# Where a step's four gathers stand among its TensorE tasks: all at once, or one by one behind a product

## The chip, the cores and the metric

The kernel runs on one NeuronCore of a Trainium2 chip. A core has five engines, each with a queue of its own that is worked off in order: TensorE (PE in the profile, its weight loads PEld), VectorE (DVE), ScalarE (ACT), GpSimd (POOL) and SyncE (SP). They share an on-chip memory (SBUF), the accumulators of the matmuls (PSUM) and 16 DMA engines, and wait for each other by semaphores. What counts is the device time of one execution in microseconds; the median of several runs is compared.

## The reference

Everything is float32. A layer of a graph network over 6250 nodes of 256 features and 100000 edges (to which every node's edge to itself is added) is followed by a mixture of experts:

```python
# graph layer, added to x
xn = layer_norm(layer_norm(x))
h = (xn @ W).reshape(N, 8, 32)
e = leaky_relu(a_src[src] + a_dst[dst], 0.2)          # one score per edge and head
alpha = exp(e - max over the edges of dst) / (sum over the edges of dst)
agg = segment_sum(h[src] * alpha[:, :, None], dst)
out = layer_norm(agg + xn @ W_res + bias)
x = x + out + gelu_tanh(out @ ffn_w1 + ffn_b1) @ ffn_w2 + ffn_b2      # 256 -> 1024 -> 256
# mixture of experts, added to x
t = layer_norm(x)
top_p, top_idx = top_k(softmax(t @ Wr + br), 2)       # two of eight experts
y[e] = gelu(ln_e(t) @ W1[e] + b1[e]) @ W2[e] + b2[e]  # 256 -> 1024 -> 256
x = x + sum over the two of (top_p / sum(top_p)) * y[top_idx]
```

The edges come sorted by their target `dst`; the sources `src` are random. So every edge needs the row of its source node, wherever that lies.

## The kernel before

**Edge steps.** A first part of the program writes a table `tab_s` to DRAM, one row per node: 256 features and 16 numbers from which the edge's weight comes (1088 bytes). Then the edges are worked off in 196 steps. A step has four tiles (`G = 4`) of 128 edges, one edge per partition. For each tile, `fetch` (L838 to L848) issues one gather on POOL: an indirect DMA that brings the 128 rows named by a column of `srce` into a quarter of the buffer `gs`. The pool of `gs` has four buffers, so the gathers of a step can start when `weigh`, four steps earlier, has read its buffer.

The rest of a step's work is spread over the steps behind it, so that every engine has something of another step to do. This is the list, worked from left to right once per step; the number says how many steps behind `fetch` a stage runs:

```python
    STAGES = ((sum_up, 6), (weigh, 3), (add_tiles, 4), (place, 4), (turn_spread, 1), (give, 2),
              (spread, 0), (add_nodes, 5), (fetch, 0))
```

- `spread` (DVE) makes a 0/1 matrix `oh` from each edge's place among 32 target nodes; `turn_spread` transposes it on PE (`pt`, L867); `give` (PE, `pz`, L875) multiplies it with the targets' numbers `qd`, so each edge gets its target's.
- `weigh` (DVE) reads the gathered rows: `ww` (L883), the maximum of two halves (L886) and `msg` (L887), the rows times the weights. It is the last that reads `gs`.
- `add_tiles` (PE, `pl`, L902) sums the messages of four tiles by target; behind the last step of a group of nodes, `add_nodes` (PE) and `sum_up` (DVE, `acc_lo`, `acc_hi`) add the group to the nodes' sums.

**Tasks.** Beside the edge steps runs everything that comes behind them: for nodes whose edges are all done, the residual, LayerNorm and the feed-forward network (node units); the routing and the scatter of the tokens' rows to the experts' lists in DRAM (`scatter`, L1437, two indirect DMAs per tile on POOL, each followed by a memset, L1448); and, as soon as an expert's list holds a block of 256 rows, that block's network. Each piece is a `Task` with an engine, a cost and the tasks that it depends on. `block_unit` makes an experts' block: `note` (DVE), `turn` (PE, transposes to `turned_in`), eight `up` (PE, `ph`, L1018, followed by the activation `ht` on ACT, L1021), eight `down` (PE, `py`, L1028), `finish` (DVE, `yb`, L1540), `weigh_block` (ACT) and two `give_back` (POOL, L1550), indirect DMAs that add the 128 rows of a tile to the output. `py` has one PSUM buffer, held from the first `down` to `finish`. Its weights (`w1b`, `w2b`, 1 MB each) and its rows `xb` are loaded by SP. The list `blocks` gets an entry for each experts' block when its tasks are made.

**What sets the order.** The whole loop is traced under `tc.manual_schedule()`: an engine's queue has its instructions in the order in which the Python code emits them. Once per step the stages are emitted, and then `run_tasks` (L974 to L991) hands out tasks in the order of `pending` until the budgets are used up, `ROOM = {"PE": 7.5, "DVE": 7.6, "ACT": 5.0, "POOL": 2.6, ...}` in microseconds, less what the stages take (`EDGES`, `BEHIND`). A POOL task costs 2.6, so that there is at most one in a step. As `fetch` is the last stage, POOL's queue has, for each step, the four gathers and then the step's POOL task, if there is one. Between the engines only data and free buffers set the order: a gather waits for nothing of its own step.

Of the kernel before, what the change touches and what calls it, by code (L numbers as in the profile page):

```python
# [45 lines left out]
F32 = mybir.dt.float32  # L46
# [8 lines left out]
P = 128  # L55
# [6 lines left out]
G = 4  # L62
# [160 lines left out]
def gnn_moe_kernel(  # L223
# [28 lines left out]
    nc = tc.nc  # L252
# [5 lines left out]
    KD = D // P  # L258
    KF = F // P
# [4 lines left out]
    DT = D + 2 * H  # L264
# [6 lines left out]
    while EP < ET:  # L271
        m = 8
# [16 lines left out]
    order = [(q, i) for q in range(NQ - 1, -1, -1) for i in range(groups[q][1])]  # L289
# [47 lines left out]
    tab_s = dp.tile([NP + P, DT], F32, name="tab_s")  # L337
# [20 lines left out]
    srce = gp.tile([P, EP], I32, name="srce")  # L358
# [126 lines left out]
    with ExitStack() as actx:  # L485
# [42 lines left out]
        for i in range(2):  # L528
# [3 lines left out]
                                    axis=AX.X, op=ALU.add)  # L532
# [26 lines left out]
        for k in range(KD):  # L559
            nc.tensor.matmul(pb.rearrange("p a h -> p (a h)"), ones,  # L560
                             gb[:, k].rearrange("p a h -> p (a h)"), start=k == 0,
                             stop=k == KD - 1)
# [24 lines left out]
        for i0, t0 in enumerate(starts):  # L587
# [16 lines left out]
            for j in range(n):  # L604
                t = t0 + j
# [14 lines left out]
                ph = aps.tile([P, WC], F32, name="ph")  # L620
                for k in range(KD):
                    nc.tensor.matmul(ph, xt[:, j, k, :], wc[:, k, :], start=k == 0,
                                     stop=k == KD - 1)
# [16 lines left out]
            for tab, r0, r1 in ((tab_q, 0, LOWR), (tab_h, HB, NP // 4)):  # L640
                a0, a1 = max(m0, r0), min(m1, r1)
                if a0 < a1:
                    nc.gpsimd.dma_start(tab[a0 - r0:a1 - r0], bass.AP(
                        tensor=tab_d.tensor, offset=tab_d.offset + a0 * 4 * 2 * H,
                        ap=[[4 * 2 * H, a1 - a0], [1, W32 * 2 * H]]))
# [3 lines left out]
            for a, k0, b0, b1 in ((acc_lo, 0, t0, min(t1, KHI + 2)),  # L649
                                  (acc_hi, KHI, max(t0, KHI + 2), t1)):  # L650
                if b0 < b1:
                    m, i = b1 - b0, slice(b0 - t0, b1 - t0)
# [172 lines left out]
    bg = edges.enter_context(tc.tile_pool(name="bg", bufs=4))  # L825
# [5 lines left out]
    live = {}  # L831

    def step_tiles(s, a):
# [2 lines left out]
        t0, m = groups[q]  # L836
        return a[:, t0:t0 + G * m].rearrange("p (j m) -> p j m", m=m)[:, :, i]

    def fetch(s):
        gs = bg.tile([P, G, DT], F32, name="gs")  # L840
        q, i = order[s]
        t0, m = groups[q]
        for j in range(G):
            t = t0 + j * m + i
            nc.gpsimd.indirect_dma_start(  # L845
                out=gs[:, j, :], out_offset=None, in_=tab_s,
                in_offset=bass.IndirectOffsetOnAxis(ap=srce[:, t:t + 1], axis=0))
        live[s, "gs"] = gs  # L848

    def spread(s):  # L850

# [20 lines left out]
    def give(s):  # L872

        pz = bps.tile([P, G * 2 * H], F32, name="pz", bufs=2)
        nc.tensor.matmul(pz, live.pop((s, "oht")), live[order[s][0], "qd"].rearrange(  # L875
            "p j c -> p (j c)"), start=True, stop=True)
        live[s, "pz"] = pz

    def weigh(s):
# [51 lines left out]
    def sum_up(q):  # L931
# [4 lines left out]
        for b in range(2):  # L936
# [4 lines left out]


    STAGES = ((sum_up, 6), (weigh, 3), (add_tiles, 4), (place, 4), (turn_spread, 1), (give, 2),
              (spread, 0), (add_nodes, 5), (fetch, 0))
    LASTST = 6

# [26 lines left out]

    def run_tasks(s, room):  # L974

        more = True
        while more:
            more = False
            for t in list(pending):
                if (t.take in held or room[t.eng] <= 0.0  # L980
                        or any(d.step is None or d.step + gap > s for d, gap in t.deps)):
                    continue
                pending.remove(t)
                t.step = s
                room[t.eng] -= t.cost
                if t.take:
                    held.add(t.take)
                if t.free:
                    held.remove(t.free)
                t.fn()  # L990
                more = True  # L991

    def back(tasks, n):

        return tasks[-n:][:1] if len(tasks) >= n else []
# [18 lines left out]
    def up(c, env, w1, func, b):  # L1014
        W = env["n"] * P
        ph = cps.tile([P, 2 * P], F32, name="ph", bufs=2)
        for k in range(KD):
            nc.tensor.matmul(ph[:, :W], w1[:, k, c * P:(c + 1) * P], env["in"][:, k, :W],  # L1018
                             start=k == 0, stop=k == KD - 1)
        ht = cw.tile([P, 2 * P], F32, name="ht", bufs=2 * KF)  # L1020
        nc.scalar.activation(ht[:, :W], ph[:, :W], func, bias=b[:, c:c + 1], scale=1.0)  # L1021
        env["ht", c] = ht

    def down(j, c0, c1, env, w2):
        if j == 0 and c0 == 0:
            env["py"] = cps.tile([P, 2, D], F32, name="py")
        for c in range(c0, c1):
            nc.tensor.matmul(env["py"][:, j, :], env["ht", c][:, j * P:(j + 1) * P], w2[:, c, :],  # L1028
                             start=c == 0, stop=c == KF - 1)

    turns, downs_, ups_ = [], [], []

# [2 lines left out]
    def net(env, src, deps, w1, w2, func, b, more=(), scale=None, more2=()):  # L1035

        n = env["n"]
        tn = task(lambda: turn(src(), "in", env, scale and scale()), "PE", 0.3 * n,
                  [*deps, *[(d, 0) for d in back(ups_, 2)]])
        free = [(d, 0) for d in back(downs_, 2)]  # L1040
        ups = [task(lambda c=c: up(c, env, w1(), func, b()), "PE", 0.46 * n, [tn, *more, *free])
               for c in range(KF)]
        dn = []
        for j in range(n):
            for c in range(0, KF, 2):
                dn.append(task(lambda j=j, c=c: down(j, c, c + 2, env, w2()), "PE", 0.92,
                               [(dn[-1], 0)] if dn else [ups[-1], *more2],
                               take=None if dn else "py"))
        if not urgent:
            before = [t for t in waiting if t.step is None]  # L1050
            for t in before:
                pending.remove(t)
            every = KF // len(before) if before else 1
            for i, t in enumerate(before):
                pending.insert(pending.index(ups[min((i + 1) * every, KF) - 1]) + 1, t)
            waiting[:] = dn
        turns.append(tn)
        ups_.append(ups[-1])
        downs_.append(dn[-1])
        return dn[-1]  # L1060
# [544 lines left out]
    blocks, stored, cleared, sure, chunked, moew, last_hi, ahead = [], [], [], [], [0], [], [], []  # L1605
# [6 lines left out]
    s, u, since, was_nodes, loaded = 0, 0, [], False, {}  # L1612

    with tc.manual_schedule():
        nc.sync.dma_start(xs[E * CAP:, :].rearrange("(p r) d -> p r d", r=2),
                          blank[:, None, :].to_broadcast([P, 2, DX]))
        while s < NG + LASTST or pending or u < len(units) or len(blocks) < NS:
# [47 lines left out]
            room = dict(ROOM if s < NG + LASTST else ROOM_AFTER)  # L1665
            if s < NG + LASTST:
                g = s - 5
                ends = 0 <= g < NG and order[g][1] == groups[order[g][0]][1] - 1
                for e in EDGES:
                    room[e] -= EDGES[e] + ends * BEHIND[e]  # L1670
            run_tasks(s, room)
            s += 1
            if there is None and final_list and final_list[0].step is not None and len(blocks) > NS - 2:
                there = nc.values_load(total[0:1, 0:1], min_val=0, max_val=NX)
        if NS < NX:
            with tc.If(there > NS):
                while pending or len(blocks) < NX:
                    nb = len(blocks) + len(ahead)
                    if len(ahead) < 2 and nb < NX:
                        block_loads(nb)  # L1680
                    if ahead:
                        block_unit(*ahead.pop(0))
                    run_tasks(s, dict(ROOM_AFTER))
                    s += 1
# [31 lines left out]
```

## Time and profile before

| | |
|---|---|
| median of 6 runs | 1831.66 us (1828.84 to 1833.26) |
| the profiled execution | 1829.86 us, span from its first to its last instruction 1828.1 us |
| PE, PEld busy | 1595.8 us (87%), 1239.2 us (68%) |
| DVE, ACT, POOL busy | 1064.8 us (58%), 707.6 us (39%), 1140.3 us (62%) |
| mean granted TensorE clock | 0.945 of full speed |
| gathers (L845) | 784, 817.3 us on POOL, 1043 ns each |
| DMA | 348.12 MB, 190 GB/s on average |

The profile is one execution on the chip. The edge steps end at about 1520 us of the span; in the steps from about the 75th on, with experts' blocks among the tasks, a step takes some 7.1 us. A line of the groups names the line of code, the engine, the operation, the program's names of the output and the inputs, how many there are, the busy time, the mean of one in ns, and the idle time of the engine just ahead of them with what ended most of it (`<-issue`: nothing that the profile shows). A line of the timeline gives the start and the duration in us; the idle time ahead stands in brackets. "DVE ww L883 <- DMA gs" in the waits reads: DVE's instruction of line 883 waited for the DMA that fills `gs`. The time that an indirect DMA takes on POOL is the time in which POOL makes its descriptors; the data land later.

### The profile page before, as it was taken

The numbers are of one execution on the slowest core, as the hardware profiler recorded it, in microseconds if no ns is written. First come the engines' busy times: TensorE is split into PE (matmuls) and PEld (weight loads), VectorE is DVE, ScalarE is ACT, GpSimd is POOL, SyncE is SP. The second block draws the span as 40 slices with busy tenths as digits, with TensorE's granted clock in tenths as the row PEclk, the third lists the DMA queues.
The fourth block names the chain that finished last, engine by engine and source line by source line (L and its number), as shares of the span: only waits on it lengthen the run. The fifth ranks groups of instructions, "written<-read, shape, count | busy, mean of one in ns | idle before, by whom it ended". The sixth has DMA issues, their size and how long they took to land. (4 is left out here: it accounts for less than half of the span.)

```text
span 1828.1 us, 28283 instructions
## 1 busy us (share of the span) xinstructions
PE 1595.8 (87%) x8479; PEld 1239.2 (68%) x8479; DVE 1064.8 (58%) x3809; ACT 707.6 (39%) x1623; POOL 1140.3 (62%) x1190
## 2 busy tenths in 40 slices
PE   5756986878787799999999999999998999999996
PEld 4533664656555577777777777777776777788885
DVE  6757878888888866675766575546344445030000
ACT  4731323233232344444444444444432343443332
POOL 4347754757666667767787777777777774222222
PEclk9977887989888899999999999999999999999998
DMA  6897644546554746667657666777676768847661
GB/s 187 263 264 246 199 142 136 152 138 173 159 155 132 234 154 199 188 183 195 202 163 222 189 191 208 212 211 222 198 223 198 228 178 252 256 110 211 186 220 40
DMA packets 246639, 348.12 MB, mean 190 GB/s; under 512 B 45992, under 2 KB 202824, under 8 KB 246476
## 3 DMA queue, kind: packets, MB, share of 16 engines
q1 hardware_dynamic: 184220, 203.16, 34.4%
q0 software_dynamic: 58944, 139.58, 28.9%
q10 hardware_dynamic: 3312, 3.48, 0.6%
q8 instruction: 70, 1.15, 0.3%
q14 instruction: 93, 0.76, 0.1%
HBM read 282.76 MB, written 67.52 MB: 192 GB/s over the span
## 5 line engine op out<-in xcount | busy, mean ns | idle before, releaser
L845 POOL DMA_INDIRECT gs<-tab_s,srce x784 | 817.3, 1043 | 331.2 <-issue 196.8
L1018 PE MATMUL ph<-turned_in,w1b 128*128 128x256 f32 (+1 forms) x1696 | 419.8, 378 | 16.6 <-ACT turned_in L1010 9.5
L1028 PE MATMUL py<-w2b,ht 128*128 128x256 f32 x1648 | 416.4, 383 | 7.7 <-DVE yb L1540 7.2
L1018 PEld LDWEIGHTS ph<-turned_in,w1b 128*128 128x128 f32 x1696 | 312.8, 191 | 67.6 <-ACT turned_in L1010 15.0
L1021 ACT ACTIVATE ht<-ph,pc 128x256 f32<-128x256 f32 (+1 forms) x424 | 197.6, 467 | 404.8 <-PE ph L1018 404.3
L1028 PEld LDWEIGHTS py<-w2b,ht 128*128 128x128 f32 x1648 | 310.5, 192 | 50.8 <-DVE yb L1540 9.0
L1550 POOL DMA_INDIRECT out_dram<-yb,tos x103 | 166.3, 1615 | 224.8 <-ACT ht L1021 80.3
L887 DVE TENSOR_TENSOR msg<-gs,msg 128x1024 f32<-128x1024 f32 x196 | 240.7, 1228 | 6.7
L1018 PE MATMUL ph<-turned_in,w_sb 128*128 128x256 f32 (+1 forms) x800 | 197.4, 388 | 3.6 <-ACT ht L1021 3.3
L1028 PE MATMUL py<-w_sb,ht 128*128 128x256 f32 x784 | 194.5, 390 | 6.1 <-DVE xin L1119 4.1
L883 DVE TENSOR_TENSOR ww<-gs,pz 128x64 f32<-128x64 f32 x196 | 42.2, 215 | 234.4 <-DMA gs<-tab_s,srce 145.7
L1028 PEld LDWEIGHTS py<-w_sb,ht 128*128 128x128 f32 x784 | 151.3, 196 | 29.1 <-DVE xin L1119 4.9
L1018 PEld LDWEIGHTS ph<-turned_in,w_sb 128*128 128x128 f32 x800 | 150.6, 198 | 28.9 <-ACT ht L1021 5.6
L1021 ACT ACTIVATE ht<-ph,prm 128x256 f32<-128x256 f32 (+1 forms) x200 | 93.2, 469 | 166.0 <-PE ph L1018 165.5
L1540 DVE TENSOR_TENSOR yb<-py,b2b 128x512 f32<-128x512 f32 (+1 forms) x53 | 35.7, 673 | 178.7 <-PE py L1028 172.4
L927 PE MATMUL p<-part,oh 128*128 128x264 f32 x220 | 82.9, 461 | 64.5 <-DVE acc_hi L938 51.8
L902 PE MATMUL pl<-msg,oh 128*32 128x264 f32 x1568 | 132.4, 410 | 6.8 <-DVE msg L887 6.7
L1437 POOL DMA_INDIRECT xs<-xe,slot x98 | 104.7, 1069 | 45.5 <-issue 19.4
L906 ACT ACTIVATE part<-pl 128x264 f32<-128x264 f32 x110 | 42.8, 389 | 195.8 <-PE pl L902 193.5
L938 DVE SCALAR_TENSOR_TENSOR acc_lo<-p,here,acc_lo 128x264 f32 x112 | 55.2, 493 | 97.9 <-PE p L927 80.6
L867 PEld LDWEIGHTS pt<-ident,oh 128*128 128x128 f32 x196 | 27.6, 141 | 115.4 <-issue 62.7
L1199 PE MATMUL py<-wres,xtf 128*128 128x256 f32 x196 | 73.3, 539 | 34.6 <-DVE rg L1205 21.5
(338 smaller groups left out, 1925.5 us busy)
## 6 DMA issues: line engine op xcount, KB each, us to landing
w1b<-in_L_ffn_W_dram SPq DMA_DIRECT2D x53, 1024.0 KB
w2b<-in_L_ffn_W_dram SPq DMA_DIRECT2D x53, 1024.0 KB
xb<-xs SPq DMA_DIRECT2D x50, 260.0 KB
gs<-tab_s,srce POOLq DMA_INDIRECT x784
b2b<-in_L_ffn_b_dram SPq DMA_DIRECT2D x53, 128.0 KB
tab_s<-hg SPq DMA_DIRECT2D x12, 544.0 KB
xg<-in_x_dram SPq DMA_DIRECT2D x12, 512.0 KB
xt_d<-xt SPq DMA_DIRECT2D x12, 512.0 KB
```

What stands on the lines that cost most here:

```text
L845: nc.gpsimd.indirect_dma_start(out=gs[:, j, :], out_offset=None, in_=tab_s, in_offset=bass.IndirectOffsetOnAxis(ap=srce[:, t:t + 1], axis=0))
L887: nc.vector.tensor_tensor(msg[:, :, :D].rearrange("p t (h d) -> p t h d", h=H), gs[:, :, :D].rearrange("p t (h d) -> p t h d", h=H), msg[: ...
L902: nc.tensor.matmul(pl[j * W32:(j + 1) * W32, :], oh[:, j, :], msg[:, j, :], start=i == 0, stop=last)
L906: nc.scalar.activation(part, pl, AF.Copy)
L927: nc.tensor.matmul(p2, oh2, part, start=True, stop=True)
L938: nc.vector.scalar_tensor_tensor(to, p2, here[:, b, q:q + 1], to, op0=ALU.mult, op1=ALU.add)
L1018: nc.tensor.matmul(ph[:, :W], w1[:, k, c * P:(c + 1) * P], env["in"][:, k, :W], start=k == 0, stop=k == KD - 1)
L1021: nc.scalar.activation(ht[:, :W], ph[:, :W], func, bias=b[:, c:c + 1], scale=1.0)
L1028: nc.tensor.matmul(env["py"][:, j, :], env["ht", c][:, j * P:(j + 1) * P], w2[:, c, :], start=c == 0, stop=c == KF - 1)
L1199: nc.tensor.matmul(py[:, j, :], env["xt"][:, j, k, :], wres[:, k, :], start=k == 0, stop=k == KD - 1)
L1437: st = nc.gpsimd.indirect_dma_start(out=xs, out_offset=bass.IndirectOffsetOnAxis(ap=slots[k][:n, t:t + 1], axis=0), in_=xes[u // 2][:n, pl ...
L1550: st = nc.gpsimd.indirect_dma_start(out=out, out_offset=bass.IndirectOffsetOnAxis(ap=tos[:, b, j:j + 1], axis=0), in_=env["yb"][:, j, :], ...
```

## The change

`fetch` emits only the first gather of a step in its place and puts the other three on a list `later`. `run_tasks` emits one of them after a task each time another quarter of the step's PE budget is used up, and what is left behind the last task. Further, each gather gets a dependency on the last product traced ahead of it (`pace[-1]`: `give`'s product, or the last matmul of an `up` or a `down`): POOL may issue it when this product is done. Both hold once `blocks` isn't empty, from step 69 on; ahead of that the four gathers are emitted at once as before, and have no such dependency. The order in which the other engines' instructions are emitted is unchanged; on POOL, a step's `give_back` or `scatter` now comes between the first gather and those behind it, wherever it is handed out ahead of them.

```diff
+    pace, later = [], []
+
     def fetch(s):
-        gs = bg.tile([P, G, DT], F32, name="gs")
+        live[s, "gs"] = bg.tile([P, G, DT], F32, name="gs")
+        gather(s, 0)
+        later.extend(lambda j=j: gather(s, j) for j in range(1, G))
+        if not blocks:
+            while later:
+                later.pop(0)()
+
+    def gather(s, j):
+
         q, i = order[s]
         t0, m = groups[q]
-        for j in range(G):
-            t = t0 + j * m + i
-            nc.gpsimd.indirect_dma_start(
-                out=gs[:, j, :], out_offset=None, in_=tab_s,
-                in_offset=bass.IndirectOffsetOnAxis(ap=srce[:, t:t + 1], axis=0))
-        live[s, "gs"] = gs
+        t = t0 + j * m + i
+        ld = nc.gpsimd.indirect_dma_start(
+            out=live[s, "gs"][:, j, :], out_offset=None, in_=tab_s,
+            in_offset=bass.IndirectOffsetOnAxis(ap=srce[:, t:t + 1], axis=0))
+        if blocks:
+            tc.add_manual_dep(ld.ins, pace[-1].name, mybir.DependencyInfo(
+                mybir.DependencyClass.Sync, mybir.DependencyReason.DATA),
+                reason="the gathers come one by one")
...
     def give(s):
...
-        nc.tensor.matmul(pz, live.pop((s, "oht")), live[order[s][0], "qd"].rearrange(
+        mm = nc.tensor.matmul(pz, live.pop((s, "oht")), live[order[s][0], "qd"].rearrange(
             "p j c -> p (j c)"), start=True, stop=True)
+        pace[:] = [mm.ins]
...
     def run_tasks(s, room):
 
+        whole = room["PE"]
...
                 t.fn()
                 more = True
+                if later and room["PE"] <= whole * len(later) / G:
+                    later.pop(0)()
+        while later:
+            later.pop(0)()
```

In `up` and `down` the last matmul is put into `pace` in the same way.

More of the change, by code (lines that the diff above doesn't have):

```diff
@@ L1017, in up @@
         for k in range(KD):
-            nc.tensor.matmul(ph[:, :W], w1[:, k, c * P:(c + 1) * P], env["in"][:, k, :W],
-                             start=k == 0, stop=k == KD - 1)
+            mm = nc.tensor.matmul(ph[:, :W], w1[:, k, c * P:(c + 1) * P], env["in"][:, k, :W],
+                                  start=k == 0, stop=k == KD - 1)
+        pace[:] = [mm.ins]
         ht = cw.tile([P, 2 * P], F32, name="ht", bufs=2 * KF)
@@ L1027, in down @@
         for c in range(c0, c1):
-            nc.tensor.matmul(env["py"][:, j, :], env["ht", c][:, j * P:(j + 1) * P], w2[:, c, :],
-                             start=c == 0, stop=c == KF - 1)
+            mm = nc.tensor.matmul(env["py"][:, j, :], env["ht", c][:, j * P:(j + 1) * P],
+                                  w2[:, c, :], start=c == 0, stop=c == KF - 1)
+        pace[:] = [mm.ins]
     turns, downs_, ups_ = [], [], []
```

## The prediction

> **What bounds the kernel now.** I read the busy times first, then four stretches of the stage that the change touches, then POOL's groups and its timeline, then the chain of events at the place where PE waits longest.
>
> The page's busy row and its row of the gathers:
>
> ```profile
> PE 1595.8 (87%) x8479; PEld 1239.2 (68%) x8479; DVE 1064.8 (58%) x3809; ACT 707.6 (39%) x1623; POOL 1140.3 (62%) x1190
> ...
> L845 POOL DMA_INDIRECT gs<-tab_s,srce x784 | 817.3, 1043 | 331.2 <-issue 196.8
> ```
>
> The stretches (window, length, then busy us and instructions of PE, PEld, DVE, ACT, POOL; then clock, DMA share, GB/s):
>
> ```profile
> 640.00:806.00 166.00, 157.89 (x892) 123.35 (x891) 113.02 (x415) 76.70 (x163) 116.42 (x117) 0.99 0.59 174
> 806.00:1140.00 334.00, 321.47 (x1811) 253.61 (x1808) 213.51 (x757) 147.98 (x320) 264.38 (x264) 0.99 0.67 200
> 1140.00:1520.00 380.00, 357.27 (x2022) 279.64 (x2021) 177.36 (x555) 145.15 (x325) 298.76 (x273) 0.99 0.71 208
> ```
>
> PE is 94 to 96% busy: it is the bound. But POOL, in the two lower rows, has hardly anything left. Its groups between 806 and 1520 us show why (busy, mean ns, then idle time before and its releasers):
>
> ```profile
> L845 POOL DMA_INDIRECT gs<-tab_s,srce x406 | 430.5, 1060 | 121.7 <-issue 105.3 <-DMA gs<-tab_s,srce 4.0 <-DVE ww L883 2.4
> L1550 POOL DMA_INDIRECT out_dram<-yb,tos x54 | 88.4, 1637 | 19.9 <-issue 10.2 <-ACT ht L1021 3.4 <-DMA out_dram<-yb,tos 2.3
> L1437 POOL DMA_INDIRECT xs<-xe,slot x38 | 40.6, 1069 | 9.4 <-issue 8.4 <-DVE rsh L468 0.3 <-DVE pc L1523 0.3
> ```
>
> Ahead of nearly every one of these 498 instructions lies the same gap, whatever releaser is named: 453 of 0.30 or 0.31 us and 38 of 0.19, behind a memset, are 143.5 of the 149 us idle by the timeline. So POOL is full from 806 to 1520: 3.4 us of real waiting, at 7 instructions, in 714. What it loses there it doesn't win back. Ahead of 806 it is not full: its last real wait is for a free buffer.
>
> ```profile
> 803.10 0.98 POOL L845 DMA_INDIRECT gs<-tab_s,srce  x1 [4.36 <-DVE msg L887]
> 804.38 1.82 POOL L845 DMA_INDIRECT gs<-tab_s,srce  x1 [0.30 <-issue]
> ```
>
> The waits between 1140 and 1520 (us in all, times, longest) show who suffers when POOL is late; from 640 to 900 us DVE has no such wait.
>
> ```profile
> DVE ww L883 <- DMA gs<-tab_s,srce: 133.7, 34, 9.8
> ...
> PE py L1028 <- DVE yb L1540: 5.8, 2, 5.1
> ```
>
> And the place where it reaches PE:
>
> ```profile
> 1381.89 0.95 POOL L845 DMA_INDIRECT gs<-tab_s,srce  x1 [0.30 <-issue]
> 1383.14 1.60 POOL L1550 DMA_INDIRECT out_dram<-yb,tos  x1 [0.30 <-issue]
> ...
> 1387.70 0.22 DVE L883 TENSOR_TENSOR ww<-gs,pz 128x64 f32<-128x64 f32 x1 [6.20 <-DMA gs<-tab_s,srce]
> ...
> 1389.52 0.68 DVE L1540 TENSOR_TENSOR yb<-py,b2b 128x512 f32<-128x512 f32 x1
> 1390.26 2.08 PE L1028 MATMUL py<-w2b,ht 128*128 128x256 f32 x4 [5.13 <-DVE yb L1540]
> ```
>
> The gather issued at 1381.89 is the fourth of step 174. weigh of that step (ww, DVE) waits for it till 1387.70; finish (yb) stands behind it in DVE's queue; PE's next down needs yb, since py has one buffer. Here a late gather is a late PE, one to one.
>
> **The change part by part.** The built order of the changed kernel has PE's, DVE's, ACT's and SP's instructions in the old order and number. On POOL two things change, from step 69 on (127 of 196 steps, 508 gathers).
>
> 1. *The waits.* A gather may not run ahead of the product traced before it. Into a step (counted from its pt, L867) the four products end at 0.5, 2.3, 4.0 and 5.2 us on average. Before, the four gathers started at -6.3, -4.9, -3.6, -2.2 us in steps 69 to 95; at +1.2 to +5.5 in 96 to 113; +0.8 to +4.9 in 114 to 138; +9.2 to +13.3 in 139 to 177; +6.7 to +10.7 behind these. So the waits bind in steps 69 to 95 and take POOL's lead away there. They are hidden at first: the data are used three steps of 7.1 us later, and DVE waits for none up to 900 us. What is lost is the lead with which POOL enters its full stretch. Step 94's first gather starts at 803.10 now; its product pz is an instruction of two parts, the second ending 806.95 + 0.33 = 807.28, and the wake-up takes 0.22 (the buffer came free at 802.88, the gather started 803.10): 807.5. **4.4 us late**, kept to the end of the full stretch less what its real waits absorb, 2.4 us at most by 1390. I take 4.4 at full, since what those six instructions wait for may come later as well. Behind step 95 the gathers come after their products anyway. Queued behind a waiting gather are the next gathers and the step's give_back or scatters; for these wait the buffers of yb (three) and the block loads on SP, for which no wait of PE shows up between 640 and 1520.
>
> 2. *The place.* A step's POOL task stood behind its four gathers and now stands between the first and the other three: a give_back in 63 of the 127 steps, a pair of scatters in 27. The three gathers are later by 1.61 + 0.31 = 1.9 us or by 2.65 (809.00 to 811.65 for a pair with its memsets); the task itself comes earlier. This doesn't add up, as POOL's sum of work is the same; it counts where PE waits. At step 174 the task is the give_back of 1383.14: **1.9 us**. Sum at 1390: 4.4 + 1.9 = 6.3 us. PE's slack behind yb there is 0.06 us, and as little at 1411.7; elsewhere from 1150 to 1330 it is 1.0 to 3.0. So stalls of some 2 us also arise earlier; they are part of the 6.3, not added, because POOL doesn't wait for PE then.
>
> 3. *The waits as instructions.* 291 more on POOL's queue, 176 more semaphore updates on PE's matmuls. A DMA on POOL has its 0.305 us gap with one, two or three waits ahead of it: nothing. up's matmuls carry updates and down's middle ones don't, and four of either take 0.86 us: nothing. Both are hidden in fixed gaps; were each wait to cost the 0.11 us between 0.19 and 0.30, POOL would be late by 32 us more at the end, which the equal gaps exclude.
>
> 4. *The clock.* Its records stand beside the stalls:
>
> ```profile
> 958.60:962.00 3.40, 1.76 (x17) 1.02 (x17) 0.71 (x2) 2.11 (x5) 2.73 (x3) 1.00 0.88 336
> 962.00:968.80 6.80, 6.80 (x22) 5.70 (x22) 3.71 (x13) 2.14 (x4) 5.03 (x6) 0.50 1.00 336
> 1385.20:1388.60 3.40, 0.00 (x0) 0.00 (x0) 0.83 (x3) 0.44 (x1) 2.73 (x3) 1.00 0.97 333
> 1388.60:1395.40 6.80, 5.14 (x12) 4.16 (x13) 2.81 (x7) 0.47 (x1) 4.63 (x4) 0.50 1.01 283
> ```
>
> A window of 3.4 us in which PE worked 1.76 was followed by 6.8 us at half clock, although no gap in it was over 1.2 us. Each 3.4 us at half clock costs 1.7 us. New stalls of 2 us may cost none of these or two, 0 to 3.4 us; only such as fall behind 1390 count. I take one, **1.7 us**, the middle. The Trainium skill ("TensorE: Matmul & The Clock Gate", section "Why this matters for your kernels") asks for no idle gap over about 3 us between bursts and has one idle window bring the half rate. By that page stalls of 2 us would cost no clock and the sum would end at 6.3; the row at 958.60 has the half rate without such a gap, so I go by the row.
>
> 5. *The stretch of the gathers.* A gather takes 0.94 us at least and 1.06 on average here, 1.4 to 2.0 where it lies beside msg (L887) on DVE: some 0.11 us each over what the fastest takes. Moving them changes which lie there, in either direction. From 96 on they keep their distance to each other except for the task, so I take 0; the ends are under the rivals.
>
> Sum: 6.3 + 1.7 = 8.0 on the profiled execution's 1829.86 us (span 1828.1): 1837.9. The median of the six runs is 1831.66, 1.8 above it: **1839.5 us**, 0.4% slower. Under 0.2% (3.7 us) a measurement can't tell it from no change.
>
> The rule that speaks most against the change is the Trainium skill's "DMA: Bandwidth & Descriptors", section "Rules for kernel authors": issue a DMA early, wait for it late. By it alone every one of the 27 steps that lose a lead of 6 us would be a loss. The trace prices this otherwise: that lead is worth nothing until POOL is full, and then 4.4 us once.
>
> **The rivals.**
>
> *Faster: POOL gets quicker.* It needs the gathers to come out from beside msg. Of the 406 gathers some 330 lie ahead of 1390 (584 of 714 us); a fall of 19 ns each pays back the 6.3 us. If a third of the 0.11 us goes, 330 x 0.037 = 12 us, POOL is 6 us earlier there, and the wait of 5.1 and its half clock (3.4) are gone: 1831.7 - 8.5 = 1823. For it: in steps 69 to 95 the gathers no longer run in bunches, and two products of a step lie 1.2 to 1.8 us apart, not 1.3 throughout. Against it: where POOL is full the waits are satisfied when they are reached, so it runs the gathers back to back as before.
>
> *No change.* The gather of 1381.89 lands 5.7 us after its issue, beside 1 MB weight loads; elsewhere it is 2.8. If 1.9 us later it lands 2.9 sooner, and the real waits absorb 2.4, then 6.3 - 2.9 - 2.4 = 1.0 is left: 1832.7. For it: a landing differs by that much from step to step. Against it: weight loads follow each other at a DMA share of 0.97 to 1.01.
>
> *Still slower.* The place costs a pair of scatters (2.65) where it decides, and the new stalls bring half clock twice over 6.8 us: 4.4 + 2.65 + 6.8 = 13.9, 1845.5.
>
> *The change does nothing.* The waits that bind are 27 steps'; were these products early enough, only the place would be left, 1.9 at a slack of 0.06: 1833.5. Against it stands the time of pz at 806.95.
>
> **How the numbers follow.** My forecast, 1835 to 1843: 0.49. Still slower, 1843 to 1850: 0.2. No change or nearly, with the change without effect, 1828 to 1835: 0.18. Faster, below 1828: 0.13. The range of 8 in 10 leaves out most of the faster case and the far end of the slower: 1828 to 1847. Faster by over 0.2% (below 1828.0) 0.13; within it (to 1835.3) 0.18; slower 0.69.
>
> **What would show it.** In the profile after: the gathers of steps 69 to 95 wait for PE's pz, ph and py, with idle time on POOL between 640 and 806 us; the first gather of step 94 starts near 807.5; from there POOL shows the same groups with the same means, and no wait for PE; DVE's waits for gathers rise from 133.7 us; PE waits for yb some 5 times, not 2, with 5.8 us growing to about 12; the end is later by the sum of these. Wrong would be: a mean gather below 1.04 us in the full stretch (then the faster case), real waits of POOL for PE behind 810 us (then pacing binds where I say it does not, and it is slower than I say), or a wait of DVE for gathers that doesn't rise.

## The result, and the profile after

The changed kernel takes **1841.27 us** (median of 22 runs, 1834.40 to 1848.61), the kernel before 1831.52 us (46 runs, 1825.67 to 1843.04). The ratio is 1.0055, with a 95% interval from 1.0042 to 1.0067: slower by some 10 us, clear of no change. Forecast were 1839.5 us, in a range from 1828 to 1847. The profiled execution of the changed kernel took 1842.32 us, with a span of 1840.5.

The busy row of the page and its row of the gathers, of the changed kernel:

```profile
PE 1601.9 (87%) x8479; PEld 1244.2 (68%) x8479; DVE 1064.5 (58%) x3809; ACT 708.0 (38%) x1623; POOL 1147.0 (62%) x1190
...
L854 POOL DMA_INDIRECT gs<-tab_s,srce x784 | 821.7, 1048 | 332.6 <-issue 149.5
```

PE does the same 8479 products, in 6 us more of busy time; the other 6 us of the longer span are waiting. Over the stretches of the change (window, length, then busy us of PE, PEld, DVE, ACT, POOL, clock, DMA share, GB/s):

```profile
640.00:806.00 166.00, 157.38 (x894) 123.06 (x893) 112.57 (x415) 77.30 (x164) 121.07 (x121) 0.99 0.59 175
806.00:1140.00 334.00, 318.81 (x1798) 251.59 (x1798) 211.70 (x750) 146.91 (x316) 261.67 (x262) 0.99 0.67 199
1140.00:1520.00 380.00, 352.23 (x1980) 275.37 (x1979) 173.35 (x540) 143.49 (x320) 294.72 (x270) 0.98 0.70 206
1520.00:1840.00 320.00, 288.98 (x1417) 245.81 (x1415) 60.63 (x267) 119.82 (x261) 84.79 (x71) 0.97 0.61 179
```

Up to 806 us PE loses nothing to speak of (157.4 busy against 157.9); from 806 to 1520 it does 55 products fewer than before in the same time (3778 against 3833). POOL is as full as it was. Its groups between 806 and 1525 us, 5 us more than in the forecast's rows of before (busy, mean ns, idle time before and its releasers):

```profile
L854 POOL DMA_INDIRECT gs<-tab_s,srce x404 | 424.2, 1050 | 122.8 <-issue 70.6 <-PE ph L1036 16.9 <-PE py L1047 7.2
L1570 POOL DMA_INDIRECT out_dram<-yb,tos x54 | 89.4, 1656 | 26.6 <-issue 9.8 <-ACT ht L1040 7.4 <-DMA out_dram<-yb,tos 4.4
```

The gathers now name PE as releaser, but their idle time is still 0.30 us each (404 x 0.30 = 121 of 122.8). The row of the give_backs (L1570) has grown from 19.9 to 26.6 us idle with the same 54 instructions: they wait. And a gather takes 10 ns less than before (1060); up to 1390 us it is 18 ns less, as shown below.

POOL's timeline around step 94, whose first gather is the one of 807.00:

```profile
803.19 0.98 POOL L854 DMA_INDIRECT gs<-tab_s,srce  x1 [0.19 <-issue]
...
807.00 0.95 POOL L854 DMA_INDIRECT gs<-tab_s,srce  x1 [0.30 <-PE p L940]
808.25 1.01 POOL L1457 DMA_INDIRECT xs<-xe,slot  x1 [0.31 <-issue]
809.26 0.12 POOL L1468 MEMSET between<- 128x1 f32 x1
809.57 1.00 POOL L1457 DMA_INDIRECT xs<-xe,slot  x1 [0.19 <-issue]
810.57 0.12 POOL L1468 MEMSET between<- 128x1 f32 x1
810.88 0.98 POOL L854 DMA_INDIRECT gs<-tab_s,srce  x1 [0.19 <-issue]
```

Before, it started at 803.10. The pair of scatters stands between the first gather and the second, as the change has it. And the place where PE waits longest, step 174's fourth gather (1391.13) and what hangs on it:

```profile
1386.52 1.60 POOL L1570 DMA_INDIRECT out_dram<-yb,tos  x1 [0.30 <-issue]
...
1391.13 0.95 POOL L854 DMA_INDIRECT gs<-tab_s,srce  x1 [0.30 <-issue]
...
1397.66 0.22 DVE L896 TENSOR_TENSOR ww<-gs,pz 128x64 f32<-128x64 f32 x1 [7.82 <-DMA gs<-tab_s,srce]
...
1399.49 0.68 DVE L1560 TENSOR_TENSOR yb<-py,b2b 128x512 f32<-128x512 f32 x1
1400.23 2.07 PE L1047 MATMUL py<-w2b,ht 128*128 128x256 f32 x4 [7.76 <-DVE yb L1560]
```

The gather is 9.2 us later than before (1381.89), PE's product 10.0 us later (1390.26).

**Where the 12 us of the profiled pair go.** The 8479 products stand in the same order in both profiles, so each can be set against itself. The changed kernel is 1.0 us ahead at 760 us. At 893 PE waits 3.44 us for `xin` (the node units' consumer of py) and then has a stretch of half clock: 4.4 behind. At 962 the kernel before has 6.8 us of half clock that the changed one hasn't: 0.8 behind. A half-clock stretch at 1100: 2.0. At 1176 a wait for yb and half clock: 6.7. At 1327: 7.8. At 1390: 9.5. At 1572 to 1600, where no gather is left, a wait of 1.95 us for yb and two more half-clock stretches: 12.8.

PE's waits from 760 us to the end for what `weigh` can hold up (us in all, times, longest), before and after:

```profile
PE py L1028 <- DVE yb L1540: 7.2, 4, 5.1
PE pl L902 <- DVE msg L887: 1.6, 1, 1.6
```

```profile
PE py L1047 <- DVE yb L1560: 13.9, 5, 7.8
PE py L1047 <- DVE xin L1139: 4.7, 2, 3.4
PE pl L915 <- DVE msg L900: 1.2, 1, 1.2
```

So PE waits 11.4 us more for the two consumers of py, and no more for the messages.

### The profile page after: what moved, and what is told of

Same layout as the page of the kernel before. It is cut to its first block, busy times and chain, and to the rows that moved or that the text cites. A ratio compares the mean times of both kernels' runs of the same rounds, so it can differ in the third digit from the quotient of the medians.

```text
span 1840.5 us, 28572 instructions
## 1 busy us (share of the span) xinstructions
PE 1601.9 (87%) x8479; PEld 1244.2 (68%) x8479; DVE 1064.5 (58%) x3809; ACT 708.0 (38%) x1623; POOL 1147.0 (62%) x1190
## 5 line engine op out<-in xcount | busy, mean ns | idle before, releaser
L1570 POOL DMA_INDIRECT out_dram<-yb,tos x103 | 166.9, 1621 | 225.8 <-ACT yb L1566 77.3
```

Source lines behind the costliest of these rows:

```text
L1570: st = nc.gpsimd.indirect_dma_start(out=out, out_offset=bass.IndirectOffsetOnAxis(ap=tos[:, b, j:j + 1], axis=0), in_=env["yb"][:, j, :], ...
```

## The experiments

All times are medians, and the kernel before was run beside each on the same chip. The first four ran on one chip, where the kernel before took 1832.5 us (35 runs).

**The place alone.** The order on POOL is the changed one; the waits are left out:

```diff
     def gather(s, j):
...
-        if blocks:
-            tc.add_manual_dep(ld.ins, pace[-1].name, ...)
```

> POOL's order as in the changed kernel (the step's give_back or scatters between the first gather and the other three), without the waits for products. Theory 'lead' (the waits of steps 69 to 95 take POOL's lead of 4.4 us, the place adds 1.9 at the end): POOL keeps its lead at step 94 (first gather again at about 803), the three later gathers are 1.9 to 2.7 us later in steps with a task, and the time is 2 to 4 us above the kernel before. Rival 'place' (the early task and what it waits for, ahead of three gathers, is nearly all of the loss): 8 to 10 us above, as the full change. Rival 'instructions' (465 waits on POOL and the updates on PE cost time wherever they stand): no difference.

Measured: 1836.09 us, ratio 1.0023 (1.0004 to 1.0042).

**The waits alone.** In `run_tasks` a POOL task is held back until the step's gathers are out; POOL has the order of before:

```diff
-                t.fn()
+                if t.eng == "POOL" and later:
+                    behind.append(t.fn)
+                else:
+                    t.fn()
...
         while later:
             later.pop(0)()
+        for f in behind:
+            f()
```

> The waits as in the changed kernel, but the step's give_back or scatters are held back behind all four gathers, as before. Theory 'lead': first gather of step 94 at about 807, POOL some 4.4 us late from there on and no wait for products behind it; 5 to 8 us above the kernel before (4.4 and one or two half-clock windows). Rival 'place': 0 to 2 us above. Rival 'instructions': 8 to 10 us above, and POOL's gaps longer than 0.30 us.

Measured: 1838.43 us, ratio 1.0036 (1.0013 to 1.0058).

**The full change in steps 69 to 95 alone, and from 96 on alone:**

```diff
-        if not blocks:
+        if not blocks or s > 95:          # the second: s < 96
             while later:
                 later.pop(0)()
...
-        if blocks:
+        if blocks and s <= 95:            # the second: s >= 96
             tc.add_manual_dep(...)
```

> The full change in steps 69 to 95 alone; from step 96 on the four gathers of a step are issued at once and wait for no product. Theory 'lead': the loss is made by step 95 and stays, 5 to 8 us above the kernel before. Rival 'place': a quarter of the steps with a task are left, 0 to 3 us above. Rival 'instructions': 108 of 465 waits are left, about 2 us above.

Measured: 1836.95 us, ratio 1.0019 (0.9996 to 1.0041).

> The full change from step 96 on alone. Theory 'lead': the waits are satisfied when POOL reaches them, so only the place is left: as the kernel with the place alone, 2 to 4 us above the kernel before. Rival 'place': 7 to 10 us above. Rival 'instructions': 369 of 465 waits, about 8 us above.

Measured: 1841.74 us, ratio 1.0056 (1.0033 to 1.0080).

What follows from the four. Place and waits cost about 0.23% and 0.36%; together 0.59%, against 0.55% for the change. Both parts are needed for the loss, so the rival that puts nearly all of it on the place falls. The early part costs less than I expected, and its interval reaches no change. The late part was expected to cost 2 to 4 us and costs 9: there theory "lead" missed, and the numbers of both rivals (7 to 10, about 8) fit. The rival "instructions" falls all the same: the place alone, without any wait, is slower, and POOL's gaps stay 0.30 us in all these profiles. That early and late part together (0.75%) come to more than the change lies within the intervals. The late part's POOL timeline shows what the theory missed:

```profile
804.94 0.98 POOL L854 DMA_INDIRECT gs<-tab_s,srce  x1 [4.36 <-DVE msg L900]
...
823.22 0.98 POOL L854 DMA_INDIRECT gs<-tab_s,srce  x1 [2.25 <-PE pz L887]
```

The first gather of step 94 still waits for its buffer, not for PE: the lead is there. It is taken 18 us later, by a pz. So nothing is settled "by step 95": POOL keeps a lead until its sum of work has used it up, and any wait for a product ahead of that point takes what is left.

The profiles of these four and of the change, each against the profile before, with the shift of PE at 760 us taken off, so that what the edit does in this stage is left (us later than before):

| | first gather of step 94 | fourth gather of step 174 | PE's product at 1390 | PE's last product |
|---|---|---|---|---|
| place alone | 0.0 | 7.3 | 8.2 | 6.0 |
| waits alone | 6.2 | 11.6 | 8.8 | 17.0 |
| steps 69 to 95 | 4.9 | 6.6 | 6.6 | 5.5 |
| from 96 on | 0.0 | 3.3 | 3.4 | 10.7 |
| the change | 4.9 | 10.2 | 10.9 | 13.7 |

In four of the five rows PE is late at 1390 by what the gather is late, within 0.9 us; with the waits alone it is 2.8 less. That agrees with the chain of the forecast: gather, ww, yb, py. The last column shows that a single profile isn't the median: the profiled run of the waits alone is the slowest of its twelve (1847.61 us). The differences between the third and the fourth column are further waits for yb and half clock behind 1390; with the late part alone PE loses 6 us between 1425 and 1450 and 2 more at 1556 to 1575.

**One wait.** All gathers as before, and a single dependency in the whole program:

```diff
+        if s == 94 and j == 0:
+            tc.add_manual_dep(ld.ins, pace[-1].name, ...)
```

> The kernel before with one wait more in the whole program: the first gather of step 94 waits for pz of its step. Theory 'lead': this gather starts near 807 us instead of 803, POOL stays 4 us late to 1520, and the time is 4 to 7 us above the kernel before, as with the waits of all steps. Rival: the waits cost by their number, one costs nothing; within 0.2% of the kernel before.

Measured: 2077.98 us beside 2072.34 for the kernel before, ratio 1.0038 (1.0009 to 1.0066). This was another chip, of which more below.

> The one added wait of step 94 again, since the first time fell on a chip on which the kernel before takes 2072 us, where ACT, DVE and PE stand still for up to 21 us at a time with no releaser in the profile. On a chip where it takes about 1832 us, theory 'lead': this gather starts near 807 us, POOL stays 4 us late to 1520, 4 to 7 us above the kernel before. Rival (the waits cost by their number): within 0.2%.

Measured, on a third chip: 2093.07 us beside 2081.27, ratio 1.0075 (1.0039 to 1.0111). Twice a program with one wait more came out slower, by 6 and by 12 us, so a loss needs no great number of waits. POOL's waits of the second, between 640 and 1520 us:

```profile
POOL gs L854 <- DVE msg L900: 94.6, 25, 9.7
...
POOL gs L854 <- PE pz L887: 15.0, 1, 15.0
```

The second row is the added wait: 15.0 us long here, 20.3 in the profile of the first time. It is more than the 4.4 expected: POOL is further ahead of PE in these profiles, and it isn't full (the row above: 94.6 us of waiting for buffers), so it can win some of it back. The figure of 4 to 7 us for a full POOL is not tested by it.

**Waits that are long satisfied.** The order of before; each gather waits for a product of two steps earlier (`made` lists the products of each step), so that the queue has 460 waits more:

```diff
+        old = made[-2] if blocks else []
+        if old:
+            tc.add_manual_dep(ld.ins, old[(j + 1) * len(old) // G - 1].name, ...)
```

> The order of the kernel before, with 460 more waits of gathers on products, spread over the four of a step, but each for a product of two steps earlier, long done when POOL arrives. Theory 'lead': POOL's gaps stay 0.30 us and the time is the kernel's before, within 0.2%. Rival 'instructions': 4 to 10 us above it.

Measured, on the second chip: 2044.77 us beside 2072.34, ratio 0.9854 (0.9802 to 0.9905). Neither expected; here the waits weren't always satisfied: POOL is at times more than two steps ahead (between 640 and 1600 us it waits 84 us for ph and 36 us for py). So the price of a satisfied wait was not measured. What there is on it are the gaps of 0.30 us in the profile after.

**weigh behind finish.** In a step in which a task that frees py is ready, `weigh` is emitted behind that task, not ahead of it; POOL's, PE's, ACT's and SP's orders stay as they are. In the kernel before, in the changed kernel, and with the waits alone:

```diff
+            ready = blocks and any(t.eng == "DVE" and t.free == "py" and ... for t in pending)
             for f, d in STAGES:
                 if 0 <= s - d < NG:
-                    f(s - d)
+                    if f is weigh and ready:
+                        later_weigh.append(s - d)
+                    else:
+                        f(s - d)
...
                 t.fn()
+                if t.eng == "DVE" and t.free == "py" and later_weigh:
+                    weigh(later_weigh.pop())
```

> The kernel before, where in steps in which a task frees py (finish, or the node units' take_up) weigh comes behind that task in DVE's queue, not ahead of it; the other queues' orders are as before. Theory 'lead' (a late gather reaches PE through yb, which stands behind ww): PE's wait of 5.1 us at 1390 and its half clock go, 5 to 8 us faster than the kernel before. Rival: the lateness reaches PE through msg and pl as soon as yb no longer carries it; within 0.2% of the kernel before.

Measured, on the second chip: 2088.18 us beside 2072.34, ratio 1.0076 (1.0048 to 1.0103). Neither number came.

> The same edit of DVE's order in the changed kernel, its gathers paced and placed as there. Theory 'lead': POOL is as late as in the changed kernel, but PE's waits for yb and the half clock behind them are gone, so it lands within 3 us of the kernel before with the same edit, some 12 to 15 us faster than the changed kernel. Rival msg and pl: 8 to 10 us above the kernel before.

Measured, together with it: 1994.40 us beside the same 2072.34, ratio 0.9617 (0.9579 to 0.9656).

> The changed kernel with weigh behind finish in DVE's queue, again. On a chip where the kernel before takes about 1832 us, theory 'lead' (lateness reaches PE through yb behind ww): PE's waits for yb and the half clock behind them are gone, 1823 to 1829, below the kernel before. Rival 'msg and pl' (it reaches PE another way): 8 to 10 us above the kernel before. If the large gain of the first time (3.8%) belongs to the edit and not to that chip, it shows here too: about 1763.

Measured, on the third chip: 2005.78 us beside 2081.27, ratio 0.9665 (0.9614 to 0.9716).

> The waits of the change with the tasks held behind the four gathers (as in the experiment with the waits alone), and weigh behind finish in DVE's queue. On a chip where the kernel before takes about 1832 us: theory 'lead' (lateness reaches PE through yb behind ww) has PE's waits for yb and the half clock behind them gone, 1823 to 1829, against 1838 for the waits alone; rival 'msg and pl': 1836 to 1842. On a chip where it takes 2030 to 2080 us: 3 to 4% faster than the kernel before if the waits are what gains there, within 1% of it if the early place of the tasks is.

Measured, on the second chip again: 1973.66 us beside 2031.92, ratio 0.9696 (0.9635 to 0.9757).

> The changed kernel itself, unedited, once more beside the kernel before. On a chip where the kernel before takes about 1832 us: 1840 to 1842 again. On one where it takes 2070 to 2080 us and the engines stand still for reasons that the profile does not show: with weigh behind finish the paced gathers were 3.4 to 3.8% faster than the kernel before there, and that edit alone 0.8% slower; if the pacing is what gains, the changed kernel is faster there too, 1990 to 2040 us; if it is the two edits together, 2070 or more.

Measured, on a fourth chip, the changed kernel without any edit: 1961.95 us beside 2037.46, ratio 0.9642 (0.9569 to 0.9716).

**What the chips have to do with it.** In the five measurements of the experiments, on four chips, the kernel before took 1832 us once and 2032 to 2081 us four times. On the slow ones the kernels with the change's waits are *faster*, the changed kernel itself, run on one of them, by 3.6%. Here the time goes elsewhere. The kernel before has no profile on such a chip; the kernel with one wait is nearly the same. Its ACT waits between 300 and 2000 us (the second time):

```profile
ACT ht L1040 <- remote: 115.7, 39, 8.2
ACT part L919 <- remote: 75.2, 12, 19.3
ACT ht L1040 <- issue: 60.9, 56, 7.9
```

Of the changed kernel on such a chip:

```profile
ACT ht L1040 <- issue: 83.7, 73, 7.8
ACT part L919 <- remote: 38.2, 4, 15.5
ACT ht L1040 <- remote: 33.1, 11, 6.5
```

"remote" and "issue" are waits for which the profile names no releasing instruction at that time. A line of the timeline of the kernel with one wait:

```profile
1062.07 0.39 ACT L919 ACTIVATE part<-pl 128x264 f32<-128x264 f32 x1 [12.38 <-remote]
```

ACT stands still for 12.38 us, and then does the next five instructions without a gap. What it waits for is PE's signal. The profile, in which the ends of products are modelled, has the product `pl` end at 1053.70; but its record of PE's semaphore has no update from 1049.07 to 1062.05, and then five within 0.25 us. ACT and DVE start behind these. All 47 remote waits of ACT over 1.5 us in this profile, and all 24 in that of the changed kernel, end with an update of that semaphore. So here PE's products are done, or are reported as done, microseconds later than the profile draws them; which of the two, it doesn't tell. Gaps over 1.5 us of both kinds between 300 and 1950 us, summed over the one profiled execution of each, beside the median time (the first one-wait execution took 2104.6 us):

| kernel | time, us | ratio to before | ACT, us | PE, us | DVE, us |
|---|---|---|---|---|---|
| before, on a chip where it takes 1832 | 1831.5 | 1 | 0 | 0 | 0 |
| changed, on such a chip | 1841.3 | 1.0055 | 0 | 0 | 5 |
| weigh behind finish | 2088.2 | 1.0076 | 290 | 80 | 86 |
| one wait, first and second time | 2078.0, 2093.1 | 1.0038, 1.0075 | 249, 247 | 68, 53 | 165, 169 |
| waits for products two steps old | 2044.8 | 0.9854 | 188 | 52 | 89 |
| changed, weigh behind finish, twice | 1994.4, 2005.8 | 0.9617, 0.9665 | 163, 168 | 35, 36 | 88, 100 |
| waits alone, weigh behind finish | 1973.7 | 0.9696 | 127 | 34 | 55 |
| changed | 1962.0 | 0.9642 | 155 | 30 | 42 |

The kernels in which the gathers are held to products stand still less, and they are the faster ones on these chips. The waits suffice for it: with the tasks back behind the four gathers (and weigh behind finish) 3.0% are still there, while the edit of DVE's order alone loses 0.8%. The place alone was not run on such a chip. What holds PE or its signals isn't settled: the packets that bring instructions take as long as on the first chip (1.1 us for 16 KB), and their ends don't precede the ends of these stops more often than chance has it. The stops lie in the time in which gathers run: the last one starts at 1520 us of the span before, and from some 1575 us on the products keep their distance to those of the first chip. The runs don't say what in the gathers does it, if they do.

So weigh behind finish says nothing of the first chip, where it was not tried. That the place of yb and xin behind weigh in DVE's queue is what passes the lateness to PE there rests on the table of the four kernels, on the timeline and on PE's waits, which grow for yb and xin and not for msg; no experiment shows it.

## Why the prediction was right or wrong

**What bounds it**: right for the chips on which the times and the profile of before were taken. POOL stayed full, with gaps of 0.30 us, and PE paid for what POOL lost.

**The waits (4.4 us)**: near in size, but not made where the forecast has it. The first gather of step 94 starts 3.9 us later, 4.9 counted from PE, which is 1.0 ahead in that run; with the waits alone it is 6.2 late. It does not wait for its own pz: that product had ended at 806.30, and the gather starts at 807.00 with the fixed gap of 0.30 us. The wait lies a step earlier, at the first gather of step 93:

```profile
799.19 0.96 POOL L854 DMA_INDIRECT gs<-tab_s,srce  x1 [1.26 <-PE pz L887]
```

Behind it the pair of scatters and three gathers run without a real wait up to 807.00. So the lead was gone a step earlier than forecast, by another product, and that 4.9 lies so near 4.4 is in part luck. Wrong was also "Behind step 95 the gathers come after their products anyway". By the forecast's own means the first gather of steps 96 to 113 came 0.7 us behind its product and the fourth 0.3; in steps 114 to 138 the fourth came 0.3 ahead of it. With the change from 96 on alone a wait of 2.25 us was left at 823.

**The place (1.9 us)**: as far as it goes, right at step 174, where the give_back now stands ahead of the gather. But the place alone made that gather 7.3 us late (3.6 us in the median time). What the sum had wrong is the term beside it: POOL's real waits, 2.4 us up to 1390, were taken to stay as they are. Beyond the fixed 0.30 us they come to 9.4 us after (give_backs 7.8, gathers 1.6): 7.0 us that the sum didn't have. With the place alone they are 8.4, all at give_backs; with the waits alone 11.8, of which 5.7 at give_backs. POOL's timeline, before and after, at one give_back:

```profile
851.16 1.61 POOL L1550 DMA_INDIRECT out_dram<-yb,tos  x1 [0.94 <-DMA out_dram<-yb,tos]
```

```profile
852.93 1.61 POOL L1570 DMA_INDIRECT out_dram<-yb,tos  x1 [3.69 <-ACT ht L1040]
```

The forecast said of the task that it "itself comes earlier", but that is not why it waits. Its rows were ready at 835.8 us, when ACT had weighed them, and POOL reaches it 7.9 us after the issue of the give_back ahead of it, in both profiles. It waits until that one has landed: issued at 842.62 and landed at 850.33 before, 7.7 us; issued at 841.64 and landed at 852.10 after, 10.5 us. (ACT's `ht`, which the row names, ended later, but no give_back reads it.) All seven such waits of give_backs after, and all five before, end 0.8 us behind the landing of the give_back ahead. POOL comes from one give_back to the next in some 7 us, so a landing that takes longer holds POOL up, and the gathers behind. Landings of 6.9 us and more are five up to 1390 in both profiles; what makes single ones long, the runs don't say.

**The waits as instructions (0)**: the gaps are unchanged, which agrees; the experiment meant to price them didn't.

**The stretch of the gathers (0)**: POOL's row of the gathers between 806 and 1390 us, before and after:

```profile
L845 POOL DMA_INDIRECT gs<-tab_s,srce x327 | 348.7, 1066 | 97.6 <-issue 83.7 <-DMA gs<-tab_s,srce 3.4 <-DVE ww L883 1.8
L854 POOL DMA_INDIRECT gs<-tab_s,srce x324 | 339.5, 1048 | 98.4 <-issue 56.2 <-PE ph L1036 12.4 <-PE pz L887 6.0
```

A gather takes 18 ns less, 5.9 us over the 323 from step 94's first to step 174's fourth, to the good. The faster rival needed 19. Put together, 4.9 + 1.9 + 7.0 - 5.9 = 7.9, and 1.9 for the scatters and the other give_backs, which took longer: 9.8. The gather was 10.2 late; the forecast had 6.3.

**PE late by what POOL is late**: right at 1390. Unforeseen was the place at 893, where the consumer of py is a node unit's `xin`, not yb. The forecast weighed PE's slack from 1150 on only, though in the profile before PE starts there within 0.15 us of xin's end. Nor did it have the wait of 1.95 us at 1572 (1582 in the profile after), which comes by another path: there yb waits for a give_back to land.

```profile
1581.84 0.69 DVE L1560 TENSOR_TENSOR yb<-py,b2b 128x512 f32<-128x512 f32 x1 [6.57 <-DMA out_dram<-yb,tos]
```

**The clock (1.7 us)**: right in kind. From 640 us on the kernel before has five half-clock stretches, in which PE works 21.7 us, the changed one seven, with 27.3: 2.8 us of loss, with stretches that fell away and others that came. They begin behind windows like these (columns as above):

```profile
892.50:895.90 3.40, 0.00 (x1) 0.01 (x1) 3.23 (x14) 0.00 (x0) 2.62 (x3) 1.00 1.00 325
895.90:899.30 3.40, 3.40 (x8) 2.77 (x9) 2.95 (x16) 0.00 (x0) 2.77 (x4) 0.50 0.74 178
...
1097.30:1100.70 3.40, 1.76 (x18) 0.93 (x16) 3.00 (x16) 2.32 (x5) 2.79 (x3) 1.00 0.88 297
```

The second kind, 1.76 us of work in 3.40 without a long gap, is the one that the forecast weighed against the Trainium skill's rule ("TensorE: Matmul & The Clock Gate", section "Why this matters for your kernels"), which speaks of idle gaps over some 3 us. The row decided rightly: 3.4 us at half clock follow at 1100.7.

**The signs**: two of those that the forecast called wrong came. POOL really waits for PE behind 810 us (at 905 and 1318, 1.2 us beyond the fixed gap). And DVE's waits for gathers between 1140 and 1520 did not rise from 133.7 us but are 106.9; over 640 to 1520 they are 142.7 against 135.6. PE's waits for yb between 1140 and 1520 grew to 10.5 us, near the 12 named, but in two waits, not five.

So the forecast's total was right while the real waits were 7 us too small in it and the gathers' stretch 6 us too large; that the sum came so close is luck in part. Of the rivals, "the change does nothing" (1833.5) and "no change" (1832.7) lie below the interval (1839.2 to 1843.8 on 1831.52), "still slower" (1845.5) above it. "Faster" came true on another chip, and with weigh behind finish on two more, by something that I hadn't named and that no row of the profile before could show.

## What to carry to other kernels

An engine that is full turns any lead that is taken from it, anywhere ahead, into lateness that stays; look for the last real wait on it, and price a new wait there. The real waits of a full queue are a term of the sum, too: look up what each ends with (here the landing of the DMA ahead, 3.7 to 10.5 us after its issue) and how near the others are to waiting. And a verdict of half a per cent from one kind of chip can turn into its opposite on another, so repeat it on several.

## What the runs showed of the hardware

On three of four chips the engines stood still at times without a releaser that the profile names, ACT for 247 to 290 us in all with gathers issued as far ahead as buffers allow, and for 127 to 188 us with gathers held to PE's products; no such gap on ACT or PE on the first chip. ACT's remote waits ended with updates of PE's semaphore, in the line shown 8.4 us behind the product's end as the profile models it. One of the chips gave 2072 us for the kernel before at one time and 2032 at another. A wait more on a DMA that POOL issues adds nothing to its gap of 0.30 us when it is satisfied. A give_back took 3.7 to 10.5 us to land after, and the next one was held for it. Half clock came behind a 3.4 us window with 1.76 us of work in it as well as behind one with none.
